# Two of v's products pulled forward among the output products, and other orders at both ends, in a two-layer graph attention kernel

## The chip, the cores and the metric

The kernel runs on one core of a Trainium2 chip. The metric is the device time of one execution in microseconds (us). The kernel before takes 2949.26 us, the median of three runs (2947.75 to 2949.96); the profiled execution took 2948.42 us, its trace spans 2946.6 us and the granted TensorE clock was 0.990 of full speed.

## What is computed

The input `x` holds 128 graphs of 128 nodes with 512 features, `adj` a mask of 128 x 128 for each graph, all in float32. Two layers follow each other, each an attention over the masked neighbours, an output product, a residual addition and a layer norm:

```python
# layer 0: 4 heads of 64, no norm ahead
sim  = where(adj, q @ k.T / 8, -max)          # q, k, v = x @ Wq, x @ Wk, x @ Wv
x    = layernorm(x + softmax(sim) @ v @ Wo + bo)
# layer 1: 8 heads of 64, on h = layernorm(x) * gamma + beta
sc   = where(adj | eye, q @ k.T / 8, -1e9)    # q, k, v = split(h @ w_qkv.T)
x    = layernorm(x + softmax(sc) @ v @ w_out.T + b_out)
```

## The kernel before

**Groups and turns.** Two graphs make a group, so there are NG = 64 groups. A group passes through both layers in several turns. `step(s)`, called for s = 2 to 67, is one turn, and works on six groups at once: layer 0's q, k and v of group s, layer 0's scores of group s-1, its probabilities times values and its output product of group s-2, layer 1's q and k of group s-2 and v of group s-3, layer 1's scores of group s-3, and layer 1's output product of group s-4. In each turn the scores come twice, once for each graph of the group (k = 2s and k = 2s + 1); I call these the first and the second half of the turn. The schedule is written by hand: the pools reorder nothing, and every engine runs its instructions in the order in which `step` names them.

**Seven products.** Each matrix product of a group is done in Strassen's way (in Winograd's form): seven products of half-size blocks in place of eight. `product(kind, g, i)` (line 321) does product i for "qk" or "v" of layer 1, `product_0` (line 377) for layer 0, `out_product` (line 414) the output product. `INTO` says which of three PSUM banks, "a", "c" or "f", product i adds to. Products 1, 6, 7 and 4 add up in "a" one after the other, and after each of them a reader takes the running sum away: ScalarE copies after 1, 6 and 5 (line 347) and 4 (line 349), VectorE adds after 2, 3 and 7 (line 352). The next product into the bank has to wait for that reader. The sums of the left blocks (`halves_sums`, line 284) are done on GpSimd, those of the weights once, on VectorE (`combine`, lines 168 to 171).

**Banks.** Layer 1's qk and v share the banks "a" and "f" of `ps_st`, one buffer each. Layer 1's output product uses "a0" and "f0", with layer 0's product. So `p("qk", s - 2, 1)`, the first product into "a" after v's fourth, waits for ScalarE's copy of v's fourth (line 349). Scores and other short-lived outputs rotate through four buffers of `ps_mm`; the one that holds scores is free once VectorE has copied them under the mask (line 460).

**Softmax.** GpSimd fills `sm` with the least value (line 458), VectorE copies the scores in where the mask is set (460) and takes the maximum (463), ScalarE takes exponentials with their sums (`exps`, 476), VectorE takes the reciprocal (484), GpSimd multiplies (485; lines 484 and 485 are `normalised`).

**Transposes by DMA.** Activations and probabilities are transposed in 32 x 32 blocks on VectorE (`turn`, line 212, for activations; `blocks`, line 503, for probabilities), written to DRAM from the SP queue (`put`, line 197) and fetched back in the other order (`fetch`, line 203), four DMAs for each tile. `turn(0, s + 1)` and `arrive(0, s + 1)` bring in layer 0's input of the next group: line 212, lines 197 and 203, then ScalarE's copy `in_order` (line 239), then GpSimd's sums. In the second half of a turn the SP queue gets, in this order: the write of `turn(0, s + 1)`, the fetch of the first half's probabilities, the write of the second half's, the fetch of `arrive(0, s + 1)`, and the fetch of the second half's. `finish` (line 252) applies gamma and beta to layer 1's input that came this way. `direct` turns use `finish_direct` (lines 264, 269, 271) in its place, which transposes on TensorE and needs no DMA; before, these are the turns 2, 64 and 65.

**Late work.** `roots` computes the layer norm's scale and shift on GpSimd, and appends the application (`norms`, line 612, ScalarE) to the list `later` and the small tensor `ratio` (lines 586, 588, 607, 608, GpSimd) to `latest`; `flush` emits what is in a list.

The second half of an ordinary turn, cut to what the change moves (v's products are `p("v", s - 3, i)`, after six `p("v", s - 3, 6)` came ahead of it):

```python
        exps(1, k)
        if s < NG:
            p("v", s - 3, 3)
            out_sums(1, s - 4)
        flush(latest)
        out_product(1, s - 4, 1, 5, 2)
        if s < NG:
            p("v", s - 3, 7)
        out_product(1, s - 4, 6, 3)
        if not direct:
            finish(s - 2, 0)
        if s < NG:
            p("v", s - 3, 4)
        normalised(k)
        turn(0, s + 1)
```

Of the kernel before, what the change touches and what calls it, by code (L numbers as in the profile page):

```python
# [27 lines left out]
def kernel(ctx: ExitStack, tc: tile.TileContext, x, adj, wq, wk, wv, wo, bo,  # L28
# [4 lines left out]
    NG = B // G  # L33
# [20 lines left out]
    later, latest = [], []  # L54

    def flush(what=later):
        while what:
            what.pop(0)()
# [16 lines left out]
    def load(g):  # L75
        if g >= NG:
            return
        R[g] = six.tile([P, G, E], F32, tag="r", name=f"r_{g}")
        M[g] = six.tile([P, G, N], U8, tag="m", name=f"m_{g}")
        nc.sync.dma_start(R[g], x[g * G:(g + 1) * G].rearrange("b n e -> n b e"))  # L80
        nc.sync.dma_start(M[g], adj[g * G:(g + 1) * G].rearrange("b i j -> i b j"))
# [68 lines left out]
    KH = KC // 2  # L150
# [3 lines left out]
    wsqk = const.tile([P, 3, KH, 2, I1 // 2], F32, name="wsqk")  # L154
    wsv = const.tile([P, 3, KH, I1 // 2], F32, name="wsv")

    def weight_sums(w, ws):
        for c in range(KH):
            if w is w1qk:
                b11, b12 = w[:, c, :, 0], w[:, c, :, 1]  # L160
                b21, b22 = w[:, KH + c, :, 0], w[:, KH + c, :, 1]
            else:
                b11, b12 = w[:, c, 0], w[:, c, 1]
                b21, b22 = w[:, KH + c, 0], w[:, KH + c, 1]
            combine(b11, b12, b21, b22, ws[:, 0, c], ws[:, 1, c], ws[:, 2, c])

    def combine(b11, b12, b21, b22, t2, t3, t4):
        nc.vector.tensor_sub(b12, b12, b11)
        nc.vector.tensor_sub(t2, b22, b12)
        nc.vector.tensor_sub(t3, t2, b11)  # L170
        nc.vector.tensor_sub(t4, b21, t2)

    def weight_sums_0():
        combine(*(w0[:, c:c + KH, h].rearrange("p c t f -> p c (t f)") for c in (0, KH) for h in range(2)),
# [179 lines left out]
    def product_0(g, *which):  # L354

        if not 0 <= g < NG:
            return
        xT = XT[0, g].rearrange("p (h c) (b n) -> p b h c n", h=2, b=2)
        xs = XS[0, g]
        for i in which:  # L360
            left = {1: xT[:, 0, 0], 2: xT[:, 0, 1], 3: xs[:, 3], 4: xT[:, 1, 1], 5: xs[:, 0],
                    6: xs[:, 1], 7: xs[:, 2]}[i]
            right = {1: w0[:, :KH, 0], 2: w0[:, KH:, 0], 3: w0[:, KH:, 1], 4: ws0[:, 2],
                     5: w0[:, :KH, 1], 6: ws0[:, 0], 7: ws0[:, 1]}[i]
            bank, first = INTO[i]
            if i == 1:

                QKV[g] = two.tile([P, G, 2, 3, P], F32, tag="qkv0", name=f"qkv0_{g}")
            if first and bank == "c":
                ACC[0, bank] = mm_tile(f"c0_{g}")  # L370
            elif first:
                ACC[0, bank] = ps_st.tile([P, 512], F32, tag=f"{bank}0", name=f"{bank}0_{g}")
            acc = ACC[0, bank]
            todo = [(t, c) for t in range(3) for c in range(KH)]
            for n, (t, c) in enumerate(todo):
                lhsT, rhs = (right[:, c, t], left[:, c]) if t < 2 else (left[:, c], right[:, c, t])
                nc.tensor.matmul(acc[:, t * P:(t + 1) * P], lhsT, rhs, start=first and n == 0,  # L377
                                 stop=n == len(todo) - 1, skip_group_check=True)
            src = acc[:, :3 * P]

            def whole(b, h):
                return QKV[g][:, b, h].rearrange("p t n -> p (t n)")

            if i in (1, 5, 6):
                EV[0, i] = one.tile([P, 3 * P], F32, tag=f"e0_{i}", name=f"e0_{i}_{g}")
                nc.scalar.copy(EV[0, i], src)
            elif i == 4:
                nc.scalar.copy(whole(1, 0), src)
            else:
                b, h, e = {2: (0, 0, 1), 3: (0, 1, 6), 7: (1, 1, 5)}[i]  # L390
                nc.vector.tensor_add(whole(b, h), src, EV[0, e])
# [36 lines left out]
    def scores(k):  # L428
        both = members(k)
        made = []  # L430
        for l, g, b in both:
            H_ = HEADS[l]

            ps = [mm_tile(f"sc{l}_{g}_{b}_{s}").rearrange("p (k n) -> p k n", n=N) for s in range(2)]
            t = slice(b * N, (b + 1) * N)
            for h in range(H_):
                r = slice((h % 2) * D, (h % 2 + 1) * D)
                if l == 0:
                    q_, k_ = (QKV[g][r, b, h // 2, i, :] for i in range(2))
                else:  # L440
                    q_, k_ = (QK[1, g][r, i * H_ // 2 + h // 2, t] for i in range(2))
                nc.tensor.matmul(ps[h % 2][:, h // 2, :], q_, k_, start=True, stop=True)  # L442
            made.append((l, g, b, ps))
        return made
# [80 lines left out]
    def probs_arrive(k):  # L525
        if members(k):
            fetch(*SCR.pop(("p", k)))
# [25 lines left out]
    def out_sums(l, g):  # L553
        if not 0 <= g < NG:
            return
        K = HEADS[l] // 2
        so = SO[l, g] = one.tile([P, 4, K // 2, N], F32, tag=("so", "xs0")[l], name=f"so{l}_{g}")
        halves_sums(so, AT[l, g].rearrange("p b (h c) n -> p b h c n", h=2))
# [63 lines left out]
    def p(kind, g, *which):  # L622
        for i in which:
            product(kind, g, i)
# [37 lines left out]
    def step(s):  # L662
        k = 2 * s

        direct = s in (2, NG, NG + 1)
        load(s + 1)
        made = scores(k)
        masked(made, 0)
        masked(made, 1)
        exps(0, k)  # L670
        addend(0, s - 2)
        with_self(s - 2)
        p("qk", s - 3, 4)
        product_0(s, 1)
        attend(s)
        exps(1, k)
        out_sums(0, s - 2)
        if s >= NG:
            out_sums(1, s - 4)
        product_0(s, 5, 2)  # L680
        out_product(0, s - 2, 1, 5, 2)
        if s < NG:
            normalised(k)
            addend(1, s - 4)
            out_product(0, s - 2, 6)
            product_0(s, 6)
            blocks(k, 0)
            out_product(0, s - 2, 3, 7)
            stats(0, s - 2, 0)
            product_0(s, 3)  # L690
            out_product(0, s - 2, 4)
            stats(0, s - 2, 1)
            product_0(s, 7)
            p("v", s - 3, 1)
            blocks(k, 1)
            p("v", s - 3, 2)
            flush()
            p("v", s - 3, 5)
        else:
            p("v", s - 3, 1)  # L700
            out_product(0, s - 2, 6, 3)
            p("v", s - 3, 2)
            out_product(0, s - 2, 7)
            stats(0, s - 2, 0)
            p("v", s - 3, 5)
            out_product(0, s - 2, 4)
            stats(0, s - 2, 1)
            normalised(k)
            if s < NG + 3:
                addend(1, s - 4)  # L710
            flush()
            blocks(k, 0, 1)
        if not direct:
            turn(1, s - 2)
            arrive(1, s - 2)
        k += 1
        made = scores(k)
        masked(made, 0)
        if s == 2:
            weight_sums(w1qk, wsqk)  # L720
        p("v", s - 3, 6)
        product_0(s, 4)
        if s >= NG:
            p("v", s - 3, 3, 7, 4)
        if direct:
            finish_direct(s - 2)
        exps(0, k)
        masked(made, 1)
        exps(1, k)
        if s < NG:  # L730
            p("v", s - 3, 3)
            out_sums(1, s - 4)
        if s == NG + 2:
            addend(1, NG - 1)
        flush(latest)
        out_product(1, s - 4, 1, 5, 2)
        if s < NG:
            p("v", s - 3, 7)
        out_product(1, s - 4, 6, 3)
        if not direct:  # L740
            finish(s - 2, 0)
        if s < NG:
            p("v", s - 3, 4)
        normalised(k)
        turn(0, s + 1)
        probs_arrive(k - 1)
        if not direct:
            finish(s - 2, 1)
        out_product(1, s - 4, 7)
        stats(1, s - 4, 0)  # L750
        if s < NG + 2:
            blocks(k, 0, 1)
        else:
            blocks_direct(k)
        arrive(0, s + 1)
        if s < NG + 2:
            probs_arrive(k)
        p("qk", s - 2, 1)
        out_product(1, s - 4, 4)
        stats(1, s - 4, 1)  # L760
        p("qk", s - 2, 2, 5, 6)
        in_order(s + 1)
        if s != NG + 2:
            flush()
        p("qk", s - 2, 3, 7)
        if s == 2:
            weight_sums(w1v, wsv)
            weight_sums_out(1)

    opening()  # L770
    for s in range(2, NG + 4):
        step(s)


# [27 lines left out]
```

## Time and profile before

| what | value |
|---|---|
| median of three runs | 2949.26 us |
| span of the trace | 2946.6 us |
| TensorE matmul busy | 2846.1 us, 97% of the span |
| VectorE busy | 1832.0 us, 62% |
| GpSimd busy | 1752.4 us, 59% |
| ScalarE busy | 1496.9 us, 51% |
| time between the starts of two ordinary turns | 44.36 us in most, 44.39 us on average |

PE is TensorE, DVE VectorE, ACT ScalarE, POOL GpSimd, SP the engine that issues the DMAs. A name such as `va` is the output tile of v's products in bank "a", `oa` that of the output product in "a0", `qka` that of qk in "a", `sc` scores, `av` probabilities times values; L321 is line 321 of the kernel. In the timeline a row is a run of equal instructions: its start and length in us, and in brackets the idle time of the engine just before it with what ended it. Starts of PE rows can be subtracted; their ends are modelled. The average of 44.39 us is over the 59 turns whose first `av` starts between 141.15 and 2715.88 us.

### The profile page before, as it was taken

To read this page: it belongs to the slowest core of one execution; us is meant where nothing else is said; L and a number is where in the kernel's file an instruction comes from. 1 tells how busy PE (TensorE), PEld (TensorE's weight loads), DVE (VectorE), ACT (ScalarE), POOL (GpSimd) and SP (SyncE) were. 2 spreads that over 40 slices of the span, in tenths; PEclk is the share of its full clock that TensorE was granted. 3 is DMA by queue.
4 is the path that set the end of the run, shared out by engine and by line. 5 is a ranking of instruction groups with operands and counts; after the bars stand their busy time and mean duration, and the time that the engine had idled before them with its cause. 6 is when DMAs were issued, how large, how long until landed. Compare 5 with 4: busy or idle time off the path is not lost.

```text
span 2946.6 us, 63045 instructions
## 1 busy us (share of the span) xinstructions
PE 2846.1 (97%) x23289; PEld 2623.1 (89%) x23289; DVE 1832.0 (62%) x3623; ACT 1496.9 (51%) x4811; POOL 1752.4 (59%) x2439
## 2 busy tenths in 40 slices
PE   7899999999999999999999999999999999999986
PEld 7799999999989989999989989999999999999975
DVE  4566666666666666665666665666666666665643
ACT  3355555555555455454554555555555555455443
POOL 2466566566566566566666566566566566566643
PEclk9899999999999999999999999999999999999988
DMA  4344544544544544544545545545545545545421
GB/s 142 112 142 136 155 133 143 158 130 141 160 129 142 158 131 138 164 128 140 166 124 144 162 124 148 160 126 148 159 127 148 157 129 148 156 129 148 136 65 58
DMA packets 243427, 408.36 MB, mean 139 GB/s; under 512 B 40104, under 2 KB 176304, under 8 KB 243120
## 3 DMA queue, kind: packets, MB, share of 16 engines
q1 hardware_dynamic: 243120, 404.33, 46.1%
q8 instruction: 185, 3.03, 0.4%
q14 instruction: 122, 1.00, 0.1%
HBM read 206.57 MB, written 197.66 MB: 137 GB/s over the span
## 4 chain that ended last, share of the span: by engine, by line
PE 89%; ACT 3%; DVE 2%; POOL 2%; DMA 1%; issue 1%; SPq 1%; ACTq 0%; POOLq 0%; DVEq 0%
PE qka L321 15%; PE a L377 11%; PE oa L414 10%; PE va L321 8%; PE qkf L321 7%; PE f L377 6%; PE sc L442 6%; PE av L546 6%; PE of L414 6%; PE vf L321 4%; PE qkc L321 4%; PE c L377 3%; PE oc L414 3%; ACT xT L252 2%; PE vc L321 2%; DMA raw<-scr 1%
## 5 line engine op out<-in xcount | busy, mean ns | idle before, releaser
L476 ACT ACTIVATE sm<-sm,nmax 128x128 f32<-128x128 f32 x1536 | 595.1, 396 | 268.4 <-DVE nmax L463 268.4
L485 POOL TENSOR_TENSOR sm<-sm,rec 128x512 f32<-128x512 f32 (+1 forms) x256 | 370.7, 1468 | 486.8 <-DVE rec L484 486.8
L284 POOL TENSOR_TENSOR xs<-xT 128x256 f32<-128x256 f32 x256 | 187.0, 730 | 431.2 <-ACT xT L239 382.4
L460 DVE COPY_PREDICATED sm<-m,sc 128x512 f32<-128x512 uint8 (+1 forms) x512 | 269.6, 579 | 204.5 <-POOL sm L458 200.1
L567 POOL TENSOR_TENSOR r<-r,bias 128x1024 f32<-128x1024 f32 x128 | 303.3, 2369 | 7.2 <-ACT r L566 7.2
L476 ACT ACTIVATION_READ_ACCUMULATOR sm<-sm,nmax 128x1 f32 x1536 | 298.3, 194 | 0.0
L503 DVE STREAM_TRANSPOSE turned<-sm 128x512 f32<-128x512 f32 (+1 forms) x255 | 243.5, 970 | 50.7 <-POOL sm L485 50.1
L418 DVE TENSOR_TENSOR r<-oa,r 128x256 f32<-128x256 f32 x512 | 213.7, 417 | 71.8 <-PE oa L414 69.3
L321 PE MATMUL qkf<-xs,w 128*128 128x128 f32 x2048 | 251.3, 276 | 3.2 <-POOL xs L284 3.2
L321 PE MATMUL qka<-xs,wsqk 128*128 128x128 f32 x2048 | 249.7, 275 | 0.0
L463 DVE TENSOR_REDUCE nmax<-sm 128x4 f32<-128x512 f32 (+1 forms) x256 | 243.9, 953 | 8.8
L321 PEld LDWEIGHTS qkf<-xs,w 128*128 128x128 f32 x2048 | 240.5, 193 | 3.4 <-POOL xs L284 3.4
L321 PEld LDWEIGHTS qka<-xs,wsqk 128*128 128x128 f32 x2048 | 239.1, 192 | 0.0
L347 ACT COPY ev<-va 128x256 f32<-128x256 f32 x128 | 47.5, 371 | 354.8 <-PE va L321 354.8
L352 DVE TENSOR_TENSOR qk<-qkf,eqk 128x512 f32<-128x512 f32 x64 | 44.3, 691 | 295.0 <-PE qkf L321 295.0
L414 PE MATMUL oa<-wso,so 128*128 128x256 f32 x768 | 215.1, 389 | 11.7 <-DVE r L418 11.7
L284 POOL TENSOR_TENSOR so<-aT 128x128 f32<-128x128 f32 (+1 forms) x256 | 151.4, 592 | 116.8 <-ACT aT L551 106.1
L612 ACT ACTIVATE r<-r,shift,root 128x512 f32<-128x512 f32 x256 | 194.3, 806 | 50.4 <-POOL shift L601 50.4
L414 PE MATMUL of<-wo,so 128*128 128x256 f32 x768 | 210.3, 383 | 0.8 <-POOL so L284 0.8
L252 ACT ACTIVATE xT<-raw,gb 128x256 f32<-128x256 f32 x244 | 133.2, 594 | 108.9 <-PE va L321 108.6
L458 POOL MEMSET sm<- 128x512 f32 (+1 forms) x256 | 181.5, 738 | 0.8 <-DVE turned L503 0.8
L414 PEld LDWEIGHTS oa<-wso,so 128*128 128x128 f32 x768 | 142.5, 192 | 43.6 <-issue 26.2
(140 smaller groups left out, 6583.5 us busy)
## 6 DMA issues: line engine op xcount, KB each, us to landing
scrp<-turned SPq DMA_DIRECT2D x124, 768.0 KB, 4.3
pT<-scrp SPq DMA_DIRECT2D x496, 192.0 KB, 4.4
scr<-turned SPq DMA_DIRECT2D x122, 512.0 KB, 3.0
raw<-scr SPq DMA_DIRECT2D x488, 128.0 KB, 3.2
r<-in_x_dram SPq DMA_DIRECT2D x64, 512.0 KB, 3.7
out_dram<-r SPq DMA_DIRECT2D x64, 512.0 KB, 2.9
m<-in_adj_dram SPq DMA_DIRECT2D x64, 32.0 KB, 3.5
raw_r<-in_L_gnn_w_qkv_dram SPq DMA_DIRECT2D x8, 256.0 KB, 4.0
```

Of the source, the lines that this page charges most:

```text
L284: nc.gpsimd.tensor_tensor(o, a0, a1, op=op)
L321: nc.tensor.matmul(o, lhsT, rhs, start=first and n == 0, stop=n == len(todo) - 1, skip_group_check=True)
L377: nc.tensor.matmul(acc[:, t * P:(t + 1) * P], lhsT, rhs, start=first and n == 0, stop=n == len(todo) - 1, skip_group_check=True)
L414: nc.tensor.matmul(acc, left[:, c], right[:, c], start=first and c == 0, stop=c == hk - 1, skip_group_check=True)
L418: nc.vector.tensor_add(part, acc, part)
L460: nc.vector.copy_predicated(sm[:, s], mask[:, None, :].to_broadcast([P, K, N]), ps[s][:, :K, :])
L463: nc.vector.tensor_reduce(nmax, sm, AX.X, ALU.max, negate=True)
L476: nc.scalar.activation(sm[:, s, k, :], sm[:, s, k, :], AF.Exp, bias=nmax[:, s, k:k + 1], accum_out=total[:, s, k:k + 1])
L485: nc.gpsimd.tensor_tensor(sm, sm, rec[:, :, :, None].to_broadcast([P, 2, K, N]), op=ALU.mult)
L503: nc.vector.transpose(t[:, :, lo:hi, :], sm)
L567: nc.gpsimd.tensor_tensor(R[g], R[g], (bias0, bias1)[l][:, None, :].to_broadcast([P, G, E]), op=ALU.add)
L612: nc.scalar.activation(R[g][:, b], R[g][:, b], AF.Identity, bias=shift[:, b:b + 1], scale=root[:, b:b + 1])
```

## The change

It moves v's seventh and fourth products of layer 1 ahead in the second half of each ordinary turn, each between two of layer 1's output products; `finish(s - 2, 0)` goes behind the fourth product, so ScalarE's copy of it stands ahead of all four activations of `finish`; and `flush(latest)` goes behind `normalised(k)`. What the last four turns did differently is now a function of its own, `closing`, with other orders on ScalarE, VectorE and GpSimd. Turn 3 becomes `direct`; in turn 2, layer 0's exponentials of the first half go behind `attend`, and the weight sums of `w1qk` are split in two parts around `normalised`. It is meant to take waits away from TensorE: the one of qk's first product for the copy of v's fourth, and those in the first and last turns.

In each ordinary turn (4 to 63):

```diff
         exps(1, k)
-        if s < NG:
+        if not direct:
             p("v", s - 3, 3)
-            out_sums(1, s - 4)
-        flush(latest)
-        out_product(1, s - 4, 1, 5, 2)
-        if s < NG:
+        out_sums(1, s - 4)
+        out_product(1, s - 4, 1)
+        if not direct:
             p("v", s - 3, 7)
-        out_product(1, s - 4, 6, 3)
+        out_product(1, s - 4, 5)
         if not direct:
-            finish(s - 2, 0)
-        if s < NG:
             p("v", s - 3, 4)
+            finish(s - 2, 0)
+        out_product(1, s - 4, 2, 6, 3)
         normalised(k)
+        flush(latest)
         turn(0, s + 1)
```

In turns 2 and 3:

```diff
-        direct = s in (2, NG, NG + 1)
+        direct = s in (2, 3)
...
-        exps(0, k)
+        if s > 2:
+            exps(0, k)
...
         attend(s)
+        if s == 2:
+            exps(0, k)
...
         masked(made, 0)
-        if s == 2:
-            weight_sums(w1qk, wsqk)
         p("v", s - 3, 6)
         product_0(s, 4)
-        if s >= NG:
-            p("v", s - 3, 3, 7, 4)
         if direct:
+            p("v", s - 3, 3, 7, 4)
             finish_direct(s - 2)
         exps(0, k)
         masked(made, 1)
+        if s == 2:
+            weight_sums(w1qk, wsqk, combine_1)
...
         normalised(k)
+        flush(latest)
+        if s == 2:
+            weight_sums(w1qk, wsqk, combine_2)
```

`combine_1` has the first two subtractions of `combine`, `combine_2` the other two. In the last four turns (64 to 67), with what was done before under `s >= NG`:

```diff
         p("v", s - 3, 1)
         out_product(0, s - 2, 6, 3)
+        normalised(k)
         p("v", s - 3, 2)
...
         stats(0, s - 2, 1)
-        normalised(k)
-        if s < NG + 3:
-            addend(1, s - 4)
-        flush()
         blocks(k, 0, 1)
         k += 1
         made = scores(k)
-        masked(made, 0)
         p("v", s - 3, 6)
+        flush()
+        masked(made, 0)
+        if s == NG + 2:
+            masked(made, 1)
+        if s < NG + 3:
+            addend(1, s - 4)
+        if s == NG + 2:
+            addend(1, NG - 1)
         p("v", s - 3, 3, 7, 4)
-        if direct:
+        if s < NG + 2:
             finish_direct(s - 2)
         exps(0, k)
-        masked(made, 1)
+        if s < NG + 2:
+            masked(made, 1)
         exps(1, k)
-        if s == NG + 2:
-            addend(1, NG - 1)
```

TensorE's own order in the last four turns stays as it was.

## The prediction

> **What bounds the kernel now.** I read the page first, then TensorE's waits, then one turn in the timeline engine by engine, then the same points of all turns. The busy row of the page:
>
> ```profile
> PE 2846.1 (97%) x23289; PEld 2623.1 (89%) x23289; DVE 1832.0 (62%) x3623; ACT 1496.9 (51%) x4811; POOL 1752.4 (59%) x2439
> ```
>
> TensorE is the bound with 97%; about 100 us of the span are its gaps. Two rows of its waits matter:
>
> ```profile
> PE qka L321 <- ACT v L349: 38.0, 61, 3.5
> ...
> PE av L546 <- DVE sm L460: 5.2, 4, 4.0
> ```
>
> The first is the wait that the change is aimed at, once a turn. The second, four times in all, looks harmless; the timeline of the turn from 1340 to 1385 us shows what stands behind it. TensorE:
>
> ```profile
> 1364.76 1.03 PE L414 MATMUL of<-wo,so 128*128 128x256 f32 x4
> 1365.63 1.03 PE L321 MATMUL va<-wsv,xT 128*128 128x256 f32 x4
> 1366.49 1.03 PE L414 MATMUL oa<-wso,so 128*128 128x256 f32 x4
> 1368.09 2.05 PE L321 MATMUL qka<-xT,w 128*128 128x128 f32 x16 [0.57 <-ACT v L349]
> ...
> 1385.03 1.09 PE L546 MATMUL av<-pT,qkv 128*64 128x128 f32 x16 [0.22 <-DVE sm L460]
> ```
>
> A product of four takes 0.865 us from start to start. qka ought to start at 1367.36 and starts at 1368.09: 0.73 us lost. VectorE:
>
> ```profile
> 1365.83 0.42 DVE L418 TENSOR_TENSOR r<-of,r 128x256 f32<-128x256 f32 x1 [0.44 <-PE of L414]
> 1366.17 0.26 DVE L484 RECIPROCAL rec<-total 128x4 f32<-128x4 f32 x2
> 1366.34 1.25 DVE L212 STREAM_TRANSPOSE turned<-r 128x512 f32<-128x512 f32 x2
> ...
> 1368.71 1.87 DVE L503 STREAM_TRANSPOSE turned<-sm 128x512 f32<-128x512 f32 x2
> ...
> 1384.53 0.79 DVE L460 COPY_PREDICATED sm<-m,sc 128x256 f32<-128x256 uint8 x2 [3.86 <-POOL sm L458]
> ```
>
> VectorE idles until output product 3 (`of`) is done; only then come the reciprocal and the transposes behind it in its order. SP, ScalarE and GpSimd carry on from there:
>
> ```profile
> 1367.62 0.34 SPq L197 DMA_DIRECT2D scr<-turned  x1
> 1368.07 2.21 SPq L203 DMA_DIRECT2D pT<-scrp  x4
> 1370.62 0.34 SPq L197 DMA_DIRECT2D scrp<-turned  x1
> 1371.12 3.07 SPq L203 DMA_DIRECT2D raw<-scr  x4
> ```
> ```profile
> 1379.79 1.14 ACT L239 COPY xT<-raw 128x512 f32<-128x512 f32 x2 [2.74 <-DMA raw<-scr]
> ```
> ```profile
> 1381.01 0.73 POOL L284 TENSOR_TENSOR xs<-xT 128x256 f32<-128x256 f32 x1 [6.94 <-ACT xT L239]
> ...
> 1383.97 1.42 POOL L458 MEMSET sm<- 128x512 f32 x2
> ```
>
> So a second path runs beside TensorE: `of` ends, reciprocal, `turn`, `blocks`, the SP queue, the fetch of the next group, ScalarE's copy, GpSimd's sums and fill, the first masked copy, and that frees the scores' buffer for the next turn's first `av`. I read these points in 59 turns. Their means: first `av` to reciprocal 25.80 us, to the end of L212 1.43, to the end of L503 2.99, to the first issue of the fetch 0.62, to L239 7.85, to the end of the first masked copy 5.19, to TensorE 0.06: 43.94 us in all. The turn takes 44.39. All but the DMA leg repeat within 0.05 us; that leg spreads by 0.4. **The second path has only 0.45 us of slack**, and in some turns none.
>
> **What the Trainium skill says.** "TensorE: Matmul & The Clock Gate", Engine queue depths: ScalarE and VectorE are strict FIFO, TensorE can pull weight loads ahead of running matmuls. The trace agrees: the reciprocals stand ready (the exponentials ended at 1364.88) and still wait behind the add of `of`; weight loads start 0.22 us ahead of their matmuls. "DMA: Bandwidth & Descriptors", Anatomy of one DMA: a DMA's wait for a semaphore is taken on the issuing sequencer, ahead of dispatch. So the fetch of `raw` can't pass the write of `scrp` ahead of it: it is issued 0.5 us after it, and that as soon as L503 ends. The clock gate page, "What's actually happening": after an idle window of about 3.4 us TensorE falls to half its clock. The trace agrees: after 3.98 us of idling at 95.09 the 16 matmuls of `av` spread over 1.98 us in place of 1.09, after 0.77 or 0.57 us nothing shows.
>
> **The change part by part.**
>
> *v's fourth product goes forward.* New order: v3, o1, v7, o5, v4, o2, o6, o3, o7, qk1. ScalarE's copy of v4 now comes right after the exponentials (1364.88) and ends near 1365.2; qk1 is due at 1367.36. The wait goes: 0.73 us, and 0.10 us of slower restart (qka takes 1.89 us from start to start here and 1.79 elsewhere). TensorE's own path falls from 44.35 to 43.52 us.
>
> *Output product 3 comes later.* It was the seventh of this row and is the eighth: 0.865 us later from the turn's start. The path's first leg becomes 26.66 us, and nothing behind it gets shorter: VectorE, SP and GpSimd keep their order from the reciprocal on.
>
> *A new tight wait.* v4 needs VectorE's add of v7 (same bank), with one product between. The add would run from 1362.37 to 1362.79, v4's weight load is due at 1362.82. After a like add that ended at 1347.08 the load came at 1347.20 and the product took 0.08 us more. I take 0.04 us, between 0 and 0.1. It lies ahead of `of`, so on the second path. The same between o6 and o7 lies behind it, and is hidden.
>
> *flush(latest) behind normalised.* Its four GpSimd operations take 1.42 us (1359.47 to 1360.89, in idle time). Behind the two multiplications, which end near 1370.17, they push GpSimd's sums for qk's fifth product to 1371.6 to 1372.3, and TensorE would want them at 1371.7: a wait of about 0.6 us. TensorE's path becomes 43.52 + 0.6 = 44.1 us, still under the second path, so hidden.
>
> *The turn:* 43.94 + 0.865 + 0.04 = 44.85 us against 44.39: **+0.46 us, in 59 turns (4 to 62) +27 us.** Turn 63 fetches no next group and gains 0.3.
>
> *Opening.* Turn 2: aT's copy no longer stands behind four exponentials (output wait 2.44 us at 57), GpSimd's sums no longer wait for eight weight sums (3.17 us at 77); the turn ends with the fetch of group 3 and the masked copy, some 3.5 us earlier. Turn 3: the 3.48 us wait for v4's copy goes, but `finish_direct` puts eight transposes (1.4 us) on TensorE and stands, on VectorE, ahead of the masked copies of layer 1: these move from 114.5 to about 121.6, exponentials end at 127.3 in place of 120.7, and the second path, 6 us later, meets 2.6 us of slack there: +3 us. A gap of about 5 us at turn 4's `av` then costs some 2 us of half clock. Together +2 us, between -4 and +5.
>
> *Closing.* Turn 64: reciprocals and multiplications come ahead, so `blocks` ends at 2815.1 in place of 2819.1, v4 no longer waits 4.88 us, and the chain of transposes, sums, fill and masked copies to output product 6 ends at about 2829 in place of 2835.15: -6.5. Turn 65 in the same way -3.5. Turn 66: one residual addition (2.35 us on GpSimd) leaves the way of the last multiplication, but v3 and v7's adds now stand behind the masked copies: -2. Together -12, between -8 and -14.
>
> *Sum:* 2949.3 + 27 - 0.3 + 2 - 12 = 2966; I say 2965.
>
> **The rivals.**
>
> *TensorE stays the bound* (other side). If the second path gives way, because the DMA leg holds an amount fixed by earlier traffic, the turn is 44.1 us: -0.29 x 59 = -17, with the ends -10: 2922. For it: 97% busy, only four waits at `av`. Against it: the leg starts with SP's issue in every turn, and the gaps at 275 and 320 us show the path binding as soon as it is 0.5 us late. 9%.
>
> *Half and half*: the DMA leg shortens by about 0.4 us, because it now meets less of the fetch of layer 1's input ahead of it. The turn is 44.4 to 44.5, the ends take back -10: about 2945 to 2955. Against it: that fetch has landed before L212 starts. 8%.
>
> *Worse*: the wait for v7's add is 0.1 or more, or gaps at `qkf` and `av` bring the clock down now and then: 45.2 us, +48 - 10: 2987. Each gap stays under 1 us, so 8%.
>
> **How the numbers follow.** The likeliest case, 75%, spans 2954 to 2977 with the bounds of the v7 wait (0 to +6), of the opening and of the closing. Adding half of the two cases on each side, the range 2948 to 2978. Faster by over 0.2% (under 2943.4): 0.09; within: 0.08; slower (over 2955.2): 0.83.
>
> **What would show it.** The wait of qka for v L349 should be gone; `av` should wait for L460 in nearly every turn, 0.6 to 0.9 us, 40 to 50 us in all, and `qkf` for GpSimd's `xs` about 0.6 us; turns should be 44.8 us apart, first `av` to reciprocal 26.7. TensorE's gaps after turn 64's first `av` (2803 us), now 29 us, should fall under 20. It is wrong if `av` doesn't wait, or if L239 comes sooner after the issue of the fetch than 7.85 us.

## The result, and the profile after

The changed kernel takes 2966.94 us (median of four runs, 2963.22 to 2970.43) against 2949.2 us before: 1.0061 times, with a 95% interval from 1.0043 to 1.0078. The forecast was 2965. Line numbers in the views of the changed kernel are 7 higher: L328 is the product of layer 1, L421 the output product, L467 the masked copy, L465 the fill, L491 the reciprocal, L219 and L510 the transposes, L246 the copy of the next group's input, L291 GpSimd's sums, L553 `av`.

The busy row and the chain that ended last, from the page of the changed kernel (engines by share of the span):

```profile
PE 2847.0 (96%) x23297; PEld 2625.9 (88%) x23297; DVE 1820.3 (61%) x3625; ACT 1496.9 (50%) x4811; POOL 1753.7 (59%) x2439
...
PE 59%; POOL 10%; DMA 10%; DVE 10%; SPq 4%; issue 3%; ACT 2%; ACTq 0%; POOLq 0%; DVEq 0%
```

TensorE is as busy as it was, to 1 us. But the chain, followed back from the last instruction, was 89% TensorE before and is 59% now; GpSimd, DMA, VectorE and the SP queue have the rest. TensorE's waits in the changed kernel (us in total, times, longest):

```profile
PE av L553 <- DVE sm L467: 38.2, 58, 2.9
PE qkf L328 <- POOL xs L291: 27.2, 60, 0.5
```

The wait of qk's first product for the copy of v's fourth is gone from the list. In its place, and with the same 38 us, `av` waits for the masked copy, in nearly every turn. One turn of TensorE in the timeline of the changed kernel (start, length, idle time before it in brackets):

```profile
1384.23 1.03 PE L421 MATMUL oa<-wso,so 128*128 128x256 f32 x4
1385.10 1.95 PE L328 MATMUL qka<-xT,w 128*128 128x128 f32 x16
...
1387.74 1.95 PE L328 MATMUL qkc<-xT,w 128*128 128x128 f32 x16
1390.15 2.05 PE L328 MATMUL qkf<-xs,w 128*128 128x128 f32 x16 [0.45 <-POOL xs L291]
...
1402.99 1.09 PE L553 MATMUL av<-pT,qkv 128*64 128x128 f32 x16 [0.57 <-DVE sm L467]
```

`qka` follows the output product after 0.87 us, with no gap; the gaps are now at `qkf` and at `av`. VectorE in the same turn:

```profile
1384.43 0.42 DVE L425 TENSOR_TENSOR r<-of,r 128x256 f32<-128x256 f32 x1 [0.44 <-PE of L421]
1384.77 0.26 DVE L491 RECIPROCAL rec<-total 128x4 f32<-128x4 f32 x2
1384.95 1.25 DVE L219 STREAM_TRANSPOSE turned<-r 128x512 f32<-128x512 f32 x2
...
1402.49 0.78 DVE L467 COPY_PREDICATED sm<-m,sc 128x256 f32<-128x256 uint8 x2 [4.21 <-POOL sm L465]
```

As before, the reciprocal comes straight behind the add of `of`, and the masked copy straight behind GpSimd's fill. The legs of the second path, as means over the same 59 turns (in the column before, the last leg is its length where `av` did wait; the mean distance there is 0.51 us, 0.45 of it the slack):

| leg | before | after |
|---|---|---|
| first `av` to reciprocal | 25.80 | 26.66 |
| to the end of the transposes of the next group | 1.43 | 1.43 |
| to the end of the transposes of the probabilities | 2.99 | 3.00 |
| to the first issue of the fetch | 0.62 | 0.58 |
| to ScalarE's copy (the DMA leg) | 7.85 | 7.97 |
| to the end of the first masked copy | 5.19 | 5.19 |
| to TensorE's `av` | 0.06 | 0.05 |
| sum | 43.94 | 44.88 |
| distance of two turns | 44.39 | 44.88 |

Before, the sum was shorter than the turn; now it is the turn. The spans of the two traces differ by 22.0 us (2946.6 and 2968.6), and split as follows: from turn 4's `av` to turn 63's 2619.09 and 2648.15, +29.1; up to turn 4's `av` 141.15 and 145.32, +4.2; from turn 63's `av` to the end 186.4 and 175.1, -11.3.

### The profile page after: what moved, and what is told of

It is laid out like the page before. It is cut to its first block, busy times and chain, and to the rows that moved or that the text cites. A ratio compares the mean times of both kernels' runs of the same rounds, so it can differ in the third digit from the quotient of the medians.

```text
span 2968.6 us, 63001 instructions
## 1 busy us (share of the span) xinstructions
PE 2847.0 (96%) x23297; PEld 2625.9 (88%) x23297; DVE 1820.3 (61%) x3625; ACT 1496.9 (50%) x4811; POOL 1753.7 (59%) x2439
## 4 chain that ended last, share of the span: by engine, by line
PE 59%; POOL 10%; DMA 10%; DVE 10%; SPq 4%; issue 3%; ACT 2%; ACTq 0%; POOLq 0%; DVEq 0%
DMA raw<-scr 9%; PE a L384 8%; PE oa L421 8%; PE va L328 7%; POOL xs L291 6%; PE f L384 6%; PE av L553 6%; PE of L421 5%; SPq L210 4%; PE vf L328 3%; PE sc L449 3%; PE c L384 3%; DVE turned L510 3%; PE qka L328 3%; PE oc L421 3%
## 5 line engine op out<-in xcount | busy, mean ns | idle before, releaser
L467 DVE COPY_PREDICATED sm<-m,sc 128x512 f32<-128x512 uint8 (+1 forms) x512 | 270.0, 581 | 283.9 <-POOL sm L465 268.3
L291 POOL TENSOR_TENSOR xs<-xT 128x256 f32<-128x256 f32 x256 | 186.5, 729 | 355.1 <-ACT xT L246 312.5
L328 PE MATMUL qkf<-xs,w 128*128 128x128 f32 x2048 | 257.1, 279 | 27.3 <-POOL xs L291 27.2
L328 PEld LDWEIGHTS qkf<-xs,w 128*128 128x128 f32 x2048 | 239.9, 193 | 38.9 <-POOL xs L291 38.7
L328 PE MATMUL qka<-xs,wsqk 128*128 128x128 f32 x2048 | 251.4, 276 | 6.2 <-ACT eqk L354 6.2
L510 DVE STREAM_TRANSPOSE turned<-sm 128x512 f32<-128x512 f32 (+1 forms) x255 | 247.1, 970 | 12.2 <-POOL sm L492 10.5
L328 PEld LDWEIGHTS qka<-xs,wsqk 128*128 128x128 f32 x2048 | 240.6, 193 | 6.3 <-issue 6.3
L421 PE MATMUL oa<-wso,so 128*128 128x256 f32 x768 | 214.7, 389 | 12.4 <-DVE r L425 12.4
L291 POOL TENSOR_TENSOR so<-aT 128x128 f32<-128x128 f32 (+1 forms) x256 | 151.6, 592 | 112.6 <-ACT aT L558 101.9
L421 PE MATMUL of<-wo,so 128*128 128x256 f32 x768 | 210.3, 383 | 1.7 <-POOL so L291 1.7
L354 ACT COPY eqk<-qka 128x512 f32<-128x512 f32 x128 | 75.3, 589 | 215.8 <-PE qka L328 215.8
L465 POOL MEMSET sm<- 128x512 f32 (+1 forms) x256 | 181.5, 737 | 2.1 <-DVE turned L510 2.1
L354 ACT COPY eqk<-qkf 128x512 f32<-128x512 f32 x64 | 37.6, 587 | 283.6 <-PE qkf L328 283.6
```

Source lines behind the costliest of these rows:

```text
L291: nc.gpsimd.tensor_tensor(o, a0, a1, op=op)
L328: nc.tensor.matmul(o, lhsT, rhs, start=first and n == 0, stop=n == len(todo) - 1, skip_group_check=True)
L421: nc.tensor.matmul(acc, left[:, c], right[:, c], start=first and c == 0, stop=c == hk - 1, skip_group_check=True)
L467: nc.vector.copy_predicated(sm[:, s], mask[:, None, :].to_broadcast([P, K, N]), ps[s][:, :K, :])
L510: nc.vector.transpose(t[:, :, lo:hi, :], sm)
```

## The experiments

All are measured on the chip against the kernel before, whose median was 2948.6 to 2950.2 us in these series. "Turn" is the mean distance of two turns, over the 59 turns from 4 to 62.

| kernel | us | ratio to before, 95% | turn |
|---|---|---|---|
| before | 2949 | 1 | 44.39 |
| changed | 2966.9 | 1.0061 (1.0043 to 1.0078) | 44.88 |
| ordinary_alone | 2972.6 | 1.0077 (1.0062 to 1.0092) | 44.84 |
| ends_alone | 2943.0 | 0.9979 (0.9972 to 0.9986) | 44.42 |
| ratio_early | 2967.9 | 1.0059 (1.0044 to 1.0074) | 44.78 |
| after_early1 | 2916.7 | 0.9893 (0.9876 to 0.9909) | 43.96 |
| before_fill | 2945.0 | 0.9989 (0.9982 to 0.9995) | 44.36 |
| fill_twice | 2959.3 | 1.0037 (1.0024 to 1.0049) | 44.62 |
| after_fill | 2937.1 | 0.9956 (0.9941 to 0.9971) | 44.29 |
| after_fill_ratio | 2906.3 | 0.9855 (0.9841 to 0.9870) | 43.83 |
| two_fills_ratio | 2890.6 | 0.9801 (0.9786 to 0.9816) | 43.53 |
| raw_first | 2987.3 | 1.0131 (1.0116 to 1.0146) | 45.20 |
| turn3_ordinary | 2956.3 | 1.0024 (1.0015 to 1.0033) | 44.80 |
| all_three | 2880.2 | 0.9763 (0.9749 to 0.9778) | 43.54 |

### Which part of the change costs: ordinary_alone and ends_alone

ordinary_alone is the kernel before with the ordinary turn's diff alone, in turns 3 to 63; ends_alone is the changed kernel with that diff undone for turns 4 to 63, here cut to what changes:

```diff
-        out_product(1, s - 4, 1)
...
-        out_product(1, s - 4, 2, 6, 3)
-        normalised(k)
-        flush(latest)
+        flush(latest)
+        out_product(1, s - 4, 1, 5, 2)
+        p("v", s - 3, 7)
+        out_product(1, s - 4, 6, 3)
+        finish(s - 2, 0)
+        p("v", s - 3, 4)
+        normalised(k)
```

> The kernel before with only the ordinary turn's part of the change (turns 3 to 63: v's seventh and fourth among the output products, the copy of v's fourth ahead of the four activations, the small ratio behind the normalisation). Theory (the second path sets the turn, and output product 3 comes 0.865 us later in it, of which 0.45 us was slack): turns 44.9 us apart instead of 44.4, +0.49 us x 59 = +29 us, so about 2978 us, more than the changed kernel as a whole. Rival (TensorE's own waits are what counts, and the loss lies in the first and last turns): the wait for the copy of v's fourth is gone, 38 us less, so about 2912 to 2922 us.

> The changed kernel with the ordinary turns (4 to 63) back in the order of before: what is left of the change is turns 2 and 3 and the last four. Theory: the turns are 44.4 us apart again and the wait of qk's first product for the copy of v's fourth is back (38 us in all); the first turns cost about +4 us and the last ones give about -11 us, so 2949 - 7 = 2942 us (2938 to 2945). Rival (the first and last turns carry the loss): 2967 us or more.

Measured: 2972.6 and 2943.0 us. The ordinary turn alone is slower than the whole change, and the first and last turns alone are faster than before. TensorE's waits in ordinary_alone:

```profile
PE av L546 <- DVE sm L460: 34.6, 54, 4.0
PE qkf L321 <- POOL xs L284: 28.6, 58, 3.2
```

and in ends_alone:

```profile
PE qka L328 <- ACT v L356: 34.5, 60, 0.6
...
PE av L553 <- DVE sm L467: 7.2, 9, 2.9
```

The pair of waits comes and goes with the ordinary turn's order, and the distance of the turns with it (44.84 and 44.42). ordinary_alone stayed 5 us under its forecast: in its trace turns 4 to 62 cost +26.4 us, and the turns ahead of them are 2.1 us shorter (139.02 us up to turn 4's `av`, for 141.15). The second need not come from the edit: fill_twice and before_fill, whose kernels have the opening of before unchanged, reach that point at 139.53 and 136.35 us.

### One wait or two: ratio_early

The small ratio tensors go back ahead of the output products in turns 4 to 63:

```diff
         out_sums(1, s - 4)
+        if not direct:
+            flush(latest)
...
         normalised(k)
-        flush(latest)
+        if direct:
+            flush(latest)
```

> The changed kernel with the small ratio tensors of GpSimd back ahead of the output products in turns 4 to 63. TensorE's wait of qk's fifth product for GpSimd's sums (27 us in all, 0.45 us each) should go in both views. Theory (the second path alone sets the turn; TensorE's wait lies beside it): av's wait for the masked copy grows by the same 0.45 us, from 38 to some 65 us in all, and the time stays at 2967 us (2963 to 2970). Rival (both waits are paid, one after the other): 2967 - 27 = 2940 us.

Measured: 2967.9 us, no different from the change. In the list of waits of ratio_early the one for `xs` has gone, and `av` has this row:

```profile
PE av L553 <- DVE sm L467: 74.8, 61, 2.9
```

38.2 us have become 74.8, which is more than the 65 expected: a wait at `qkf` costs more than its 0.45 us in the list (see after_fill). What TensorE saved at `qkf` it waited at `av`: while the second path sets the pace, a wait that lies beside it is free.

### Where the second path starts: after_early1

`normalised`, `flush(latest)` and `turn` go ahead of layer 1's output product 3:

```diff
-        out_product(1, s - 4, 2, 6, 3)
+        out_product(1, s - 4, 2, 6)
         normalised(k)
         flush(latest)
         turn(0, s + 1)
+        out_product(1, s - 4, 3)
```

> The changed kernel with the reciprocals, the multiplication, the small ratio tensors and the transposes of the next group ahead of layer 1's output product 3 instead of behind it (turns 4 to 63). It tests where the second path starts. Theory (VectorE takes its work in order, so the reciprocal stands behind the add of output product 3): the reciprocal comes 0.87 us earlier, at 25.8 us of the turn; the transposes of the probabilities, with that add now ahead of them, some 0.45 us earlier; the wait for GpSimd's sums goes as well, and the turn takes 44.43 us, -0.45 x 59 = -27 us: 2940 us (2932 to 2945). Rival (what starts the second path is something else, the exponentials or the fill): 2960 us or more.

Measured: 2916.7 us, nearly twice the gain forecast. VectorE in the timeline of after_early1:

```profile
1356.06 0.42 DVE L425 TENSOR_TENSOR r<-oa,r 128x256 f32<-128x256 f32 x1 [0.44 <-PE oa L421]
1356.40 0.26 DVE L491 RECIPROCAL rec<-total 128x4 f32<-128x4 f32 x2
1356.57 1.25 DVE L219 STREAM_TRANSPOSE turned<-r 128x512 f32<-128x512 f32 x2
1357.74 0.39 DVE L425 TENSOR_TENSOR r<-of,r 128x256 f32<-128x256 f32 x1
```

The reciprocal now follows the add of output product 6 (`oa`), and its mean start is 25.80 us into the turn: 0.86 earlier, as expected. So it is the place in VectorE's order that started the path, not the exponentials. The legs are 25.80 + 1.43 + 3.20 + 0.60 + 7.69 + 5.18 + 0.07 = 43.97, and the turn takes 43.96. The expectation went wrong in the third leg: I gave the add that moved into it 0.4 us, and it lengthened the leg by 0.20 (3.20 for 3.00). The DMA leg also came out 0.28 shorter (7.69 for 7.97), which none of the runs explains.

### How much slack there was: before_fill and fill_twice

before_fill is the kernel before with GpSimd's fill of layer 0's scores tile for the next turn taken ahead of the sums of the next group, so that the masked copy no longer stands behind the fetch; fill_twice does that fill twice in 58 turns, where it stood. `filled` makes the tile and fills it, and `masked` takes a tile from `FILLED` if there is one. The diffs of before_fill and of fill_twice, cut:

```diff
+        if 4 <= s < NG - 1:
+            FILLED[0, s, 0] = filled(0, s, 0)
         in_order(s + 1)
```

```diff
             nc.gpsimd.memset(sm, (NEG0, NEG1)[l])
+            if l == 0 and b == 0 and 4 <= g < NG - 2:
+                nc.gpsimd.memset(sm, (NEG0, NEG1)[l])
```

> The kernel before with GpSimd's fill moved ahead in the same way. Theory (there TensorE was the bound, with 0.45 us of slack on the second path, which it lost in a few turns only): the mean turn goes from 44.39 to 44.34 us, -3 us: 2944 to 2949 us, against -30 us from the same edit in the changed kernel. Rival (the second path binds before too): -20 us or more.

> The kernel before with GpSimd's fill of the first half's layer 0 scores tile done twice in 58 turns: 1.42 us more on the second path, and on nothing else that TensorE waits for. It measures the slack. Theory (slack 0.45 us of 44.39): the turns get 1.42 - 0.45 = 0.97 us longer, 45.36 us, +56 us: 3005 us. Rival (no slack: +1.42 x 58): 3032 us. Rival (2 us of slack or more): 2949 us.

Measured: 2945.0 and 2959.3 us. The first is as expected: without the second path the kernel before runs at 44.36 us, all of it TensorE's, so the path cost it 0.03 us a turn. The second is far off its number, and the dose is why. GpSimd in the timeline of fill_twice:

```profile
2591.57 0.53 POOL L458 MEMSET sm<- 128x512 f32 x1
2592.15 0.53 POOL L460 MEMSET sm<- 128x512 f32 x1
2592.61 0.95 POOL L458 MEMSET sm<- 128x1024 f32 x1
```

Layer 0's fill takes 0.53 us. The 1.42 that I doubled was the row of two fills run together, layer 0's and layer 1's. The leg from ScalarE's copy to the end of the masked copy grew from 5.19 to 5.77, by 0.58, and the turn from 44.39 to 44.62. With 0.45 us of slack on average, a dose of 0.58 leaves 0.13 a turn, and the DMA leg spreads by some 0.4: if that spread is taken as normal, the mean of the excess, where only what is above zero counts, is an estimated 0.23 us. TensorE's 44.36 and 0.23 give 44.59; 44.62 was measured. So a slack of 0.45 fits; with the dose of 0.58, no slack would have meant 44.97 us and a slack of 2 us 44.39.

### What the order is worth without the second path: after_fill, after_fill_ratio, two_fills_ratio

The same edit as in before_fill, in the changed kernel; then with the ratio tensors early as well; then with layer 1's fill too:

```diff
         if 4 <= s < NG - 1:
             FILLED[0, s, 0] = filled(0, s, 0)
+            FILLED[1, s - 2, 0] = filled(1, s - 2, 0)
         in_order(s + 1)
```

> The changed kernel with one thing moved: GpSimd fills the first half's layer 0 scores tile of the next turn ahead of the sums of the next group's input instead of behind them, so the first masked copy no longer stands behind the fetch of the next group. Theory (the fetch reaches TensorE only through that fill): the wait of av for the masked copy (38 us in all) goes, the fetched input is still in time for layer 0's products (2 us of slack), and a turn takes TensorE's own 43.52 us plus the 0.45 us wait for GpSimd's sums: 43.97 us, 0.91 less than 44.88, x 59 = -54 us: about 2913 us. Rival (another link, such as the fetched input itself or the exponentials, binds next at nearly the same place): -10 us or less, 2955 to 2967 us.

> The changed kernel with both: GpSimd's fill ahead of the sums of the next group, and the small ratio tensors back ahead of the output products. With the fill moved alone the turns were 44.29 us apart and TensorE had one wait left in each, qk's fifth product for GpSimd's sums. Theory (TensorE is the bound now, so this wait is paid in full, with the 0.2 to 0.3 us around it that the list of waits doesn't count: the product ahead of it took 2.41 us instead of 1.78 and the next 1.89 instead of 1.79, 0.73 us together): 43.55 us a turn, -0.73 x 59 = -43 us from 2937: 2894 us. Rival (only the 27 us of the list of waits): 2910 us. Rival (another wait takes its place, as the second path did before): 2930 us or more.

> The changed kernel with the small ratio tensors ahead of the output products and both fills of the next first half, layer 0's and layer 1's, ahead of the sums of the next group. With layer 0's fill alone moved, the turns were 43.79 us apart on average, 43.51 at best, and in 20 of them layer 1's av waited for the masked copy behind layer 1's fill (0.95 us), which still stood behind the fetch. Theory (that fill is the last link between the fetch and TensorE's bank): all turns at 43.5 us, -0.28 x 59 = -16 us from 2906: 2890 us. Rival (the fetched input itself binds next): 2900 us or more.

Measured: 2937.1, 2906.3 and 2890.6 us. One fill of 0.53 us, moved, takes 30 us off the changed kernel and 4 off the kernel before. That is the clearest sign that the fetch of the next group reached TensorE through the fill, and that the bound had changed.

after_fill gained 30 where 54 was expected. Its turns were steady at 44.29 us, with the wait at `qkf` as the only one in a usual turn. TensorE in after_fill, and after it in all_three, where that wait is gone:

```profile
1368.96 1.95 PE L328 MATMUL qkc<-xT,w 128*128 128x128 f32 x16
1371.37 2.05 PE L328 MATMUL qkf<-xs,w 128*128 128x128 f32 x16 [0.46 <-POOL xs L291]
1373.26 1.95 PE L328 MATMUL qka<-xs,wsqk 128*128 128x128 f32 x16
```

```profile
1381.55 1.95 PE L328 MATMUL qkc<-xT,w 128*128 128x128 f32 x16
1383.33 1.95 PE L328 MATMUL qkf<-xs,w 128*128 128x128 f32 x16
1385.12 1.95 PE L328 MATMUL qka<-xs,wsqk 128*128 128x128 f32 x16
```

From `qkc` to the second `qka` it is 4.30 us with the wait and 3.57 without: a wait that is listed with 0.46 us costs 0.73 (the last section says why). I had counted 0.45.

after_fill_ratio stayed at 43.83 us a turn where 43.55 was expected (the 43.79 quoted above leaves out turn 4, which took 45.68). The list of waits has 14 waits of `av` for the masked copy, 10.0 us in all, where two_fills_ratio keeps 2, of 3.2 us together; so layer 1's `av` waited visibly in a dozen turns rather than 20. GpSimd and VectorE in one of them (with the fill moved, L462 is the fill and L475 the masked copy):

```profile
2426.86 0.95 POOL L462 MEMSET sm<- 128x1024 f32 x1
```

```profile
2427.84 1.37 DVE L475 COPY_PREDICATED sm<-m,sc 128x512 f32<-128x512 uint8 x2 [3.79 <-POOL sm L462]
```

Layer 1's fill still stood behind the fetch, and it holds up layer 1's masked copy. With it moved too the turns take 43.53 us: TensorE's own 43.52 of the prediction.

### The SP queue's order: raw_first

```diff
+        if not direct:
+            arrive(0, s + 1)
         blocks(k, 0, 1)
-        arrive(0, s + 1)
+        if direct:
+            arrive(0, s + 1)
         probs_arrive(k)
```

> The changed kernel with the four fetches of the next group's input issued ahead of the write of the probabilities instead of behind it (turns 4 to 63). The fetch then doesn't wait for the transposes of the probabilities, and its first issue comes some 0.8 us earlier. Theory (the second path sets the turn through the SP queue's order): the turn gets shorter by up to 0.6 us, after which TensorE with its wait for GpSimd's sums binds at 44.29: 2931 to 2945 us. Rival (the fetch's 8 us are spent on waiting for its own write and on DMA engines shared with the other fetches, so that an earlier issue lands no earlier): 2960 us or more.

Measured: 2987.3 us. That lies in the rival's range, but not for the rival's reason. The queue and TensorE in the timeline of raw_first:

```profile
2389.98 1.73 SPq L210 DMA_DIRECT2D raw<-scr  x4
2392.43 0.34 SPq L204 DMA_DIRECT2D scrp<-turned  x1
2398.38 1.89 SPq L210 DMA_DIRECT2D pT<-scrp  x4
```

```profile
2404.22 0.66 PE L553 MATMUL av<-pT,qkv 128*64 128x128 f32 x8 [1.17 <-DMA pT<-scrp]
```

The fetch does land earlier: from the end of the transposes to ScalarE's copy 0.23 + 6.38 us, against 0.58 + 7.97. But the write of the probabilities now waits in the queue behind four fetches, and their own fetch follows it by 5.95 us. It is issued 4.0 us ahead of the next turn's first `av`; in the changed kernel it was 7.6. The second half of `av` waits for it: 42.5 us in 49 turns. So there is a third path, of the probabilities through DRAM, that was hidden by less than was given away here.

### The first turns, and all together: turn3_ordinary and all_three

```diff
-        direct = s in (2, 3)
+        direct = s == 2
```

turn3_ordinary has only this on top of the change, all_three this and two_fills_ratio.

> The changed kernel with turn 3 as an ordinary turn again (its layer 1 input by DMA instead of through TensorE, the exponentials not behind the activations of finish_direct). Theory: turn 3 lasted 53.3 us against 46.1 before, with a wait of 6.16 us of a qk product for a copy behind the exponentials; that wait goes, and the turn takes 45 to 48 us: 2967 - 7 = 2960 us (2957 to 2963). Rival (the waits belong to the first turns' fetches and come back elsewhere): 2966 us or more.

> The changed kernel with the small ratio tensors and both fills moved and turn 3 as an ordinary turn. Theory: the gains of the two add up, 2890 - 7 = 2883 us. Rival (turn 3's gain is lost in the turns after it, which then wait for their fetch): 2890 us.

Measured: 2956.3 and 2880.2 us. Turn 3 in the timeline of the changed kernel, TensorE and ScalarE:

```profile
119.79 1.95 PE L328 MATMUL qkf<-xs,w 128*128 128x128 f32 x16
127.90 3.33 PE L328 MATMUL qka<-xs,wsqk 128*128 128x128 f32 x14 [6.16 <-ACT eqk L354]
```

```profile
124.08 0.40 ACT L483 ACTIVATE sm<-sm,nmax 128x128 f32<-128x128 f32 x1 [5.56 <-DVE rec L491]
...
127.19 0.56 ACT L354 COPY eqk<-qka 128x512 f32<-128x512 f32 x1
```

VectorE, in the same turn:

```profile
121.38 1.33 DVE L467 COPY_PREDICATED sm<-m,sc 128x512 f32<-128x512 uint8 x2 [4.10 <-POOL sm L465]
```

ScalarE's copy out of bank "a" stands behind eight exponentials, and these wait for layer 1's masked copy and its maximum. The masked copy in turn waits for GpSimd: VectorE's part of `finish_direct` has ended at 117.28, but GpSimd then does the four sums of `finish_direct` (117.43 to 120.45) and only behind them layer 1's fill (0.95 us from 120.39). So it is a fill behind sums here too. As an ordinary turn, turn 3 takes 44.2 us in place of 53.3. The gain of 10.7 us is larger than the 7 expected, which were taken from the one trace of before (46.1 us for turn 3; before_fill and fill_twice have 43.2 and 44.1 for it). all_three adds the two gains up. Its busy row, and its chain:

```profile
PE 2822.8 (98%) x23289; PEld 2616.1 (91%) x23289; DVE 1834.8 (64%) x3623; ACT 1508.5 (52%) x4811; POOL 1765.3 (61%) x2439
...
PE 95%; DVE 1%; POOL 1%; ACT 1%; issue 1%; DMA 0%; SPq 0%; ACTq 0%; POOLq 0%; DVEq 0%
```

The chain is TensorE again, 95% of it. This version, the change with the fills and the ratio tensors moved and turn 3 mended, is 2.4% faster than the kernel before and 2.9% faster than the changed one.

## Why the prediction was right

*Two paths, 0.45 us of slack.* Shown: ratio_early (a TensorE wait of 27 us removed, nothing gained), before_fill against after_fill (-4 and -30 us for one edit), and fill_twice for the size. Two readings of the legs were not exact: the leg to the first issue of the fetch also spreads, by 0.24 us (standard deviation) and not by 0.05, and the 0.06 us to TensorE was not a mean (0.51) but the length where `av` waits. The slack of 0.45 stands, as the difference of the two.

*The wait for v's fourth goes, and TensorE's own turn is 43.52 us.* Shown: the row is gone, and with the other waits moved out of the way the turn takes 43.53.

*Output product 3 comes 0.865 us later, and nothing behind it gets shorter.* Shown: 26.66 for 25.80, the other legs as they were but for 0.08 us more between the transposes and ScalarE's copy, a stretch that spreads by 0.4 from turn to turn. after_early1 takes the 0.86 back by the position in VectorE's order.

*v4's wait for v7's add, 0.04 us.* It does not show: 26.66 - 25.80 is 0.86, the product itself.

*flush(latest) makes `qkf` wait some 0.6 us, hidden.* It is 0.45 by the list, and hidden, as ratio_early shows. Hidden by less than it looked: it costs 0.73, so TensorE's own turn in the changed kernel is 44.29 (after_fill) and not 44.1. Of the 0.83 us that the order of v's products takes off TensorE's turn, this edit alone gives 0.73 back.

*The turn: 44.85, +27 us.* 44.88, and +29.1 us. The waits of `av` came to 38.2 us, a little under the 40 to 50 forecast, and the DMA leg did not get shorter (7.97 for 7.85), which would have been the sign against it.

*The opening: +2.* This was forecast too small. The pair of traces has +4.2, but one pair is not enough here: three traces have the opening of before (before, before_fill, fill_twice), and in them turn 4's `av` comes at 136.4 to 141.2 us, 139.0 on average; in the eight that have the opening of the changed kernel it comes at 143.0 to 146.8, 144.5 on average. So the opening costs some 5.4 us. Within one order the times follow the granted clock, which from turn 2's `av` to turn 4's is 0.94 in before_fill, 0.90 in fill_twice and 0.89 in before (86.2, 88.7 and 90.5 us). Turn 2 gained about 4 us (40.1 to 40.4, for 43.0 to 44.6), as forecast. What went wrong is turn 3, which was to lose 3 us and some 2 by half clock behind it, and lost about 9 (52.5 to 54.9, for 43.2 to 46.1). The masked copies behind `finish_direct` were foreseen, and the time too (121.38 for 121.6), but not what holds them up (GpSimd's sums and fill, not VectorE's order) nor who waits: I expected a gap of 5 us at turn 4's `av`; it was 6.16 us at a qk product and 2.94 at `av`.

*The closing: -12.* -11.3: turn 64 -7.1 (-6.5 forecast), turn 65 -3.7 (-3.5), turn 66 -0.1, which was to give 2, and -0.3 in the turns 63 and 67 together. In turn 66 the wait for the last multiplication fell from 5.5 to 1.8 us, but v4's wait for the add of v7 grew from 1.6 to 4.7 us: the price of the adds behind the masked copies was set too low. TensorE's gaps after turn 64's first `av` fell from 29.4 to 22.3 us, not to under 20: two of about 6 us for the adds of output products stayed (at 2861 and 2904 us). Of the other 4 us, 2.8 are products that had run slowly behind a gap: in turn 64 before, the four steps from the wait of 4.88 us on took 6.35 us (2822.83 to 2829.18) where the changed kernel, with a wait of 1.45 there, takes 3.57. The rest was not followed up.

*The half clock.* After the 6.16 us wait the qk product of turn 3 ran slowly: the row above shows the 14 of its matmuls that start before 131 us, where that view ends, and all 16 spread over 3.76 us; 16 take 1.95 elsewhere. "TensorE: Matmul & The Clock Gate", section "What's actually happening", of the Trainium skill says that an idle window of about 3.4 us halves the clock; this agrees. But the length of a wait alone does not decide it here: in turn3_ordinary a wait of 2.57 us was followed by a qk product that spread over 3.85 us, while after the 2.94 us at turn 4's `av` in the changed kernel `av` took its usual 1.09. The waits of under 1 us in every turn cost no clock: from turn 4's `av` to turn 63's the granted clock is 1.00 in both kernels.

The sum was 2966, put at 2965; the medians say 2966.9. The four runs spread from 2963 to 2970, so the closeness of the two is partly luck: the traces' parts sum to +22.0, where I had +16.7 over 2949.3.

## What to carry to other kernels

Before taking out a short wait that a busy engine has in every turn, look for a second chain that comes round to the same engine, and add up its legs over many turns: the removal pays only as far as that chain has slack, and an order that starts it later can cost more than the wait did. A wait that the list shows only a few times can mark a path with little slack. And an operation that depends on nothing in the chain (here a fill of half a microsecond) should not be queued behind it; take it out first, then reorder.

## What was not expected of the hardware

A short wait of TensorE costs more than the list of waits says, and the rows above show why. At `qkf` it is 0.73 us for a listed 0.46, at `qka` 0.83 us (44.36 - 43.53) for the listed 0.57 of the turn shown in the prediction. The list counts from the modelled end of the row before: that of `qkc` is 1.95 us long, while the next product usually starts 1.78 us after it, so 0.17 us of lost time lie under that row and are not counted (1.03 and 0.865 in the case of `qka`, again 0.17). That part is a matter of the list and not of the chip. The other 0.10 us is real: the product behind the gap takes 1.89 us to the next one instead of 1.79. What makes it slower was not tried. Steps from start to start, with and without the wait, give the whole price.

In this queue a fetch that reads back what was just written follows the write's issue by some 6 us (2392.43 to 2398.38 in raw_first, and 1389.22 to 1395.36 in the changed kernel), and the trace has that write of 768 KB landing 6.1 us after its issue. From the first of the four fetches to the landing of the last it is another 5.8 us in the changed kernel and 5.7 in raw_first (means over the 59 turns). So the write's turnaround makes up half of the third path from the queue on, and raw_first put its start back.
